# Gate/up integers in two DRAM tiles, stored by ScalarE, and subtracted in turn by VectorE and GpSimd

## The chip, the cores and the metric

The kernel runs on one core of a Trainium2 chip. The core has TensorE (PE, matrix multiplication), VectorE (DVE), ScalarE (ACT), GpSimd (POOL) and SyncE (SP, which mostly issues DMAs), and sixteen DMA engines that carry out what any of them issues. A DMA is issued by an instruction in the queue of one engine, and signals a semaphore when it has landed.

The metric is the time of one execution in device microseconds. Times are compared as medians of several executions. Line numbers such as L371 are lines of the kernel before the change.

## What is computed

Four layers are applied to 2 x 512 tokens of width 512, each as `x = x + layernorm(layer(layernorm(x)))`: a Mamba block (projections, a short convolution, a scan over 512 steps with 16 states for 1024 channels), a gated feed-forward layer whose weights are packed in 4 bits, an attention with one key and value head, and a feed-forward layer with latent experts. The change touches the unpacking of the second layer's weights. In the reference they are

```python
def dequant_gptq(qweight, scales, zeros, groupsize):
    K = qweight.shape[0] * PACK          # PACK = 8 nibbles along K
    q = qweight[k // PACK, :] >> (k % PACK * 4)[:, None] & 15
    z = zeros[:, n // PACK] >> (n % PACK * 4)[None, :] & 15
    zp = (z.astype(jnp.float32) + 1.0) * s
    return q.astype(jnp.float32) * s[g] - zp[g]        # g = k // 128
...
gate = x2 @ Wg                # 512 -> 1376
up = x2 @ Wu
inter = gate * jax.nn.sigmoid(gate) * up
out = (inter @ Wd).astype(jnp.float16)                 # 1376 -> 512
```

## The kernel before, in words

**Stages.** The two sequences are called batch 0 and batch 1. The Mamba scans of both batches fill the span up to about 566 us, with VectorE and GpSimd as the busy engines. Then come, in this order: the out-projection of batch 1 (`po`, L1334, 32 matmuls); the down-projection of batch 0's feed-forward layer (`fo`, L1353, 88 matmuls in 44 ticks, each with a weight pair `wd0_j` loaded from `wd_d`); then `gptq(1)`, the gate, up and down-projection of batch 1, beside which `chain(0)` (norm and attention of batch 0) runs; then the attention of batch 1 and the latent layer of both batches up to the end.

**Packed weights.** An int32 word of `gate_q` or `up_q` holds eight 4-bit numbers along the contraction dimension. Partition p of a tile holds one of 64 rows of words of gate (p below 64) or up, so that one nibble number j gives 128 rows of weights. For batch 0 the weights are fully dequantized during the scan (`wgu_d`). For batch 1 only the integers minus their zeros are made ("whole words") and written to a DRAM tile `wgi_d`; their scales `gus` are applied when the products leave PSUM, in `evict` of gptq.

**Whole words (L353 to L376).** The 1376 columns are cut at CUTS into 512, 512 and 352. For each cut and each j: VectorE takes the nibble out (L239), ScalarE casts the integers to float in place (L368), GpSimd subtracts the zeros (L370), SyncE stores the word (L371) into `wgi_d`, in the order "r a k n -> k r a n", so that the outermost of the destination's dimensions is k with 4 entries. The tile `q` has three buffers: the nibble of word k + 3 waits for the store of word k. The first two cuts are spawned 24 ticks into the stage; the third is spawned beside gptq(1).

**Weights from DRAM.** `gu_weights` (L391) loads `wg` and `wu` in strips of 256 columns from `wgi_d` through `w4` (L114). A load waits for the stores that wrote the columns it reads. `down_words` (L335) makes the weights of the down-projection and stores them to `wd_d`; `head_sums` (L378) sums the query weights over the heads.

**Norms.** `normed_job(i)` (L1280) takes the out-projection of token tile i of batch 1 through two layer norms, and asks TensorE for a transposition (`tp_f`, L1310) that is answered between matmuls of `fo`; `split` then makes the two parts `hhi` and `hlo` that gptq(1) multiplies.

**What sets the order.** `run(stream)` advances the stream that yields matmuls, and after each matmul one tick of all spawned jobs; a job that yields n sleeps for n ticks. The order of instructions on PE, ACT, DVE and POOL is pinned to the order in which they are made; the order of SyncE's queue is decided by the scheduler. The completion semaphores of DMAs of SyncE and ScalarE are eight lanes that are handed out in turn, and a DMA waits for the one before it on its lane. Consequently an instruction that waits holds everything behind it in its engine's queue.

Of the kernel before, what the change touches and what calls it, by code (L numbers as in the profile page):

```python
# [9 lines left out]
F32 = mybir.dt.float32  # L10
F16 = mybir.dt.float16
F32R = mybir.dt.float32r
I32 = mybir.dt.int32
# [6 lines left out]
P = 128  # L20
B = 2
S = 512
# [29 lines left out]
PW = 2 * P  # L52
NP = (INTER + PW - 1) // PW
CUTS = [(0, 2), (2, 4), (4, NP)]


@with_exitstack
def tile_sandwich(
# [129 lines left out]


    wgu_d = dram.tile([P, 2, KH, INTER], F32, tag="wgu", name="wgu_d")  # L190
    wgi_d = dram.tile([P, 2, KH, INTER], F32, tag="wgi", name="wgi_d")
    wd_d = dram.tile([INTER, H], F32, tag="wd", name="wd_d")
    wfe_d = dram.tile([P, KH, LAT], F32, tag="wfe", name="wfe_d")

# [43 lines left out]
    def nibble(q, qw, j):  # L238
        nc.vector.tensor_scalar(q, qw, 4 * j, 15, ALU.logical_shift_right, ALU.bitwise_and)  # L239

    class GateUpWords:
# [73 lines left out]
        def word(self, eng=nc.vector):  # L315
            for _ in self.steps(eng):
                pass
# [16 lines left out]
    def down_words(d, dq, loaded):  # L334

        nr = INTER // PACK
        m, hw = nr - P, H // 2
        qw, z, s, r, n = loaded
        wd_v = wd_d.rearrange("(r e) n -> e r n", e=PACK)
        for j in range(PACK):  # L340
            q = dq.tile([P, S], I32, tag="q", name=f"q_d{d}_{j}", bufs=2)
            nibble(q[:r, :n], qw[:r, :n], j)
            w = dq.tile([P, S], F32, tag="w", name=f"w_d{d}_{j}", bufs=3)
            nc.vector.tensor_sub(w[:r, :n], q[:r, :n], z[:r, :n])
            nc.gpsimd.tensor_mul(w[:r, :n], w[:r, :n], s[:r, :n])  # L345
            if d == 0:
                nc.sync.dma_start(out=wd_v[j, :P, :], in_=w[:, :H])
            else:
                for a in range(2):
                    nc.sync.dma_start(out=wd_v[j, P:nr, ts(a, hw)], in_=w[a * m : (a + 1) * m, :hw])  # L350
            yield 2 - j % 2

    def whole_words(a, iq):  # L353

        n0, n1 = CUTS[a][0] * PW, min(CUTS[a][1] * PW, INTER)
        n = n1 - n0
        qw = iq.tile([P, CW], I32, tag=f"qw{a}", name=f"qw_w{a}")
        z = iq.tile([P, CW], F16, tag=f"z{a}", name=f"z_w{a}")
        parts = [(i, src, 0, KH * RG, None, zd) for i, (src, zd) in enumerate(zip((gate_q, up_q), zds))]
        word_loads(parts, n0, n1, qw, z, None, 2, nc.sync, nc.sync)  # L360

        def words():
            for j in range(PACK):
                q = iq.tile([P, CW], I32, tag="q", name=f"q_w{a}_{j}", bufs=3)
                nibble(q[:, :n], qw[:, :n], j)
                yield 1
                w = q.bitcast(F32)
                nc.scalar.copy(w[:, :n], q[:, :n])  # L368
                yield 1
                nc.gpsimd.tensor_sub(w[:, :n], w[:, :n], z[:, :n])  # L370
                nc.sync.dma_start(  # L371
                    out=wgi_d[j * RG : (j + 1) * RG, :, :, n0:n1].rearrange("r a k n -> k r a n"),
                    in_=w[:, :n],
                )
                yield 1

        return words()

    def head_sums(dq):

        wqs = [(w48[:, k, 0:HD], Wq[ts(k, P)]) for k in range(KH)]
        wqs.append((b48[:, 0:HD], bq.partition_broadcast(P)))
        for i, (dst, src) in enumerate(wqs):
            wq = dq.tile([P, S], F32, tag="w", name=f"wq{i}", bufs=3).rearrange("p (d h) -> p d h", h=NH)
            nc.sync.dma_start(out=wq, in_=src)
            nc.vector.tensor_reduce(dst, wq, AX.X, ALU.add)
            yield 2
# [1 line left out]
    hTs, o16 = {}, {}  # L389

    def gu_weights(b, j):  # L391
        src = wgi_d if b else wgu_d
        cols = slice(j * PW, min((j + 1) * PW, INTER))
        n = cols.stop - cols.start
        return [w4(src[:, a, :, cols], f"w{nm}{b}_{j}", KH, n) for a, nm in enumerate("gu")]

# [55 lines left out]
    with ExitStack() as mamba:  # L452
# [261 lines left out]
        with ExitStack() as p2:  # L714
# [24 lines left out]
            def spawn(gen, lag=0):  # L739
                jobs.append([now[0] + lag, gen])  # L740
# [535 lines left out]
        with ExitStack() as p3:  # L1276
            dq = pool(p3, "dq2", 1)

            def normed_job(i, ps):

                name = f"mo1_{i}"
                o = new_u(f"o1_{i}")
                nc.scalar.copy(o, ps)
                yield 3
                mv = moments([o], name)
                rs = rstd(mv, name, 1)
                yield 2
                nm = minus_mean(mv, rs, name, 1)
                yield 1
                apply(o, o, rs, nm, 0)  # L1290
                yield 2
                nc.vector.tensor_add(xs(1)[i], xs(1)[i], o)
                name = f"f1_{i}"
                mv = moments([xs(1)[i]], name)
                rs = rstd(mv, name, 1)
                yield 2
                nm = minus_mean(mv, rs, name, 1)
                yield 1
                xn = jrow(f"xn_{name}")
                apply(  # L1300
                    xn.rearrange("p (k j r) -> p k r j", k=KH, j=PACK),
                    xs(1)[i].rearrange("p (k r j) -> p k r j", k=KH, j=PACK), rs, nm, 0,
                )
                yield 2
                tps = []

                def turn():
                    tp = bank(f"tp_f1_{i}").rearrange("p (k t) -> p k t", k=KH)
                    for kc in range(KH):
                        nc.tensor.transpose(tp[:, kc, :], xn[:, ts(kc, P)], ident)  # L1310
                    tps.append(tp)

                def split():
                    hi, lo = (t_[:, :, ts(i, P)] for t_ in hhl)
                    nc.scalar.copy(hi, tps[0])
                    yield 1
                    nc.vector.tensor_sub(lo, tps[0], hi.bitcast(F32))

                asks.append((turn, split()))

            def words_jobs():
                yield from down_words(0, dq, down[0])
                yield from down_words(1, dq, down[1])
                yield 20
                yield from head_sums(dq)

            def outs():
                po = [obank(f"po1_{i}") for i in range(TB)]
                for j in range(NCH // 2):
                    w = wo_pair(1, 0, j)  # L1330
                    tiles = [(e, i) for e in range(2) for i in range(TB)]
                    for e, i in sorted(tiles, key=lambda ei: ei[j == NCH // 2 - 1]):
                        c = 2 * j + e
                        nc.tensor.matmul(  # L1334
                            po[i], g[1][c][:, ts(i, P)], w[:, e, :],
                            start=(c == 0), stop=(c == NCH - 1),
                        )
                        yield
                        if c == NCH - 1:
                            spawn(normed_job(i, po[i]), 1)  # L1340
                for i, m in enumerate(IC):
                    j, e = divmod(i, 2)
                    if not e:
                        w = wst.tile([P, 2, H], F32, tag="w4", name=f"wd0_{j}")
                        n = len(IC[i : i + 2])
                        nc.sync.dma_start(
                            out=w[:m, :n],
                            in_=wd_d[i * P : i * P + n * m].rearrange("(k p) h -> p k h", p=m),
                        )
                    for t in range(TB):  # L1350
                        if not i:
                            fo0.append(obank(f"fo0_{t}"))
                        nc.tensor.matmul(  # L1353
                            fo0[t], its[i][:m, ts(t, P)], w[:m, e],
                            start=(i == 0), stop=(i == len(IC) - 1),
                        )
                        yield

            def whole_jobs():
                for words in whole[:2]:  # L1360
                    yield from words

            whole = [whole_words(a, iqp) for a in range(len(CUTS))]
            fo0 = []
            spawn(words_jobs(), 1)
            spawn(whole_jobs(), 24)
            run(outs())
            while jobs or asks:
                if asks:
                    answer()  # L1370
                tick()
            pin()
# [306 lines left out]
        yield from gptq_norm(b)  # L1679
        yield from attention(b, ask)  # L1680

    spawn(whole[2], 2)
    spawn(chain(0, fo0, lambda fn, then: asks.append((fn, then))), 1)
    run(gptq(1))
    while jobs or asks:
# [77 lines left out]
```

## Time and profile before

The median of three runs is 936.14 us.

| What | Before |
|---|---|
| Runs | 937.45, 933.98, 936.14 us |
| Profiled execution's own time | 933.81 us |
| Its span | 932.0 us |
| Mean granted TensorE clock | 0.964 |
| `q_w` nibbles on VectorE, 24 | 329 / 419 / 996 ns (min, median, max) |
| `q_w` casts on ScalarE, 24 | 474 / 617 / 624 ns |
| `q_w` subtracts on GpSimd, 24 | 856 / 1153 / 1273 ns |
| `wgi_d` store issues on SyncE, 24 | 511 / 524 / 573 ns, first at 596.3, last at 696.8 us |
| `po` on TensorE | 568.3 to 595.8 us |
| First gate matmul of gptq(1), `fg` | 661.12 us |

The span is the time between the first and the last instruction that the profiler saw; the execution's own time is a little longer. Each row of a group gives the number of instructions and the duration of one. In the waits, an engine's idle time is put down to what released it last; `DMA wgi_d<-q_w` is the store of a word's tile `q_w` into `wgi_d`, and `wg<-wgi_d` the load of a strip of it. In the chain of waits each row is a piece of time with its start, its length and the work that held it. The packets of section 3 of the page count the time of all sixteen DMA engines, so that a share of 25% is a quarter of their common time.

### The profile page before, as it was taken

How to read it: one execution, taken by the hardware profiler on the slowest of the kernel's cores; microseconds unless marked ns; L12 is line 12 of the kernel's file. 1: busy time of each engine (PE TensorE's matmuls, PEld its weight loads, DVE VectorE, ACT ScalarE, POOL GpSimd, SP SyncE). 2: the span in 40 equal slices, each digit the busy share in tenths (PEclk: the TensorE clock that was granted, in tenths of full speed). 3: DMA queues.
4: the chain of work that ended last, by engine and by line, in shares of the span. 5: the costliest groups of instructions: out<-in, count | busy, mean ns of one | idle time of the engine just before them, and what ended most of it. 6: DMA issues, size and time to landing. Idle time of an engine off the chain costs nothing. (4 is left out here: it accounts for less than half of the span.)

```text
span 932.0 us, 7483 instructions
## 1 busy us (share of the span) xinstructions
PE 828.5 (89%) x2188; PEld 383.7 (41%) x2188; DVE 729.6 (78%) x859; ACT 455.7 (49%) x706; POOL 535.6 (57%) x378
## 2 busy tenths in 40 slices
PE   6988978879999899599999998986589999999995
PEld 3433433333544443244444433342346545445442
DVE  6878899999999999999999997561485964535126
ACT  4357875656676656657565540242445554310110
POOL 7757796777887788867787876543353420011002
PEclk9998999899999999899999999999799999999998
DMA  6539011010003954101101024554442231101101
GB/s 202 202 138 378 29 38 39 30 38 31 23 24 98 319 204 145 60 0 46 45 23 46 8 88 168 183 203 149 127 122 87 70 114 46 68 12 41 39 0 45
DMA packets 48018, 86.82 MB, mean 93 GB/s; under 512 B 8134, under 2 KB 22833, under 8 KB 47978
## 3 DMA queue, kind: packets, MB, share of 16 engines
q1 hardware_dynamic: 45706, 80.35, 25.5%
q0 software_dynamic: 1984, 5.47, 1.6%
q10 hardware_dynamic: 288, 0.52, 0.2%
q8 instruction: 17, 0.28, 0.1%
q14 instruction: 23, 0.19, 0.1%
HBM read 69.45 MB, written 16.88 MB: 93 GB/s over the span
## 5 line engine op out<-in xcount | busy, mean ns | idle before, releaser
L1138 POOL TENSOR_TENSOR bx<-bx,C 128x1024 f32<-128x1024 f32 x128 | 302.4, 2363 | 100.5 <-DVE bx L1132 77.8
L1132 DVE TENSOR_TENSOR_SCAN bx<-da,bx 128x1024 f32<-128x1024 f32 x128 | 291.9, 2280 | 2.3 <-ACT da L1112 2.3
L1160 PE MATMUL py<-bx,ident 128*128 128x512 f32 x480 | 232.2, 613 | 27.4 <-POOL bx L1138 23.6
L1112 ACT ACTIVATE da<-dt,A 128x511 f32<-128x511 f32 x256 | 176.6, 690 | 148.9 <-DVE bx L1132 144.4
L1128 DVE TENSOR_TENSOR bx<-du,B 128x1024 f32<-128x1024 f32 x127 | 153.1, 1206 | 2.6 <-DMA B<-scr 0.5
L1160 PEld LDWEIGHTS py<-bx,ident 128*128 128x128 f32 x480 | 91.3, 196 | 151.1 <-issue 96.4
L130 POOL TENSOR_TENSOR rs_lo<-ve_lo,mhalf 128x1 f32<-128x1 f32 x8 | 7.4, 919 | 91.4 <-DVE ve_lo L128 91.4
L780 PE MATMUL pg<-xT,w_g 128*128 128x512 f32 x114 | 56.0, 621 | 3.3 <-ACT dt L598 3.3
L1602 PE MATMUL pup<-hT_l,wup 128*128 128x512 f32 x128 | 57.7, 606 | 0.0
L1666 PE MATMUL pd<-wdn,hid 128*128 128x512 f32 x128 | 55.9, 597 | 0.0
L368 ACT CAST q_w<-q_w 128x512 f32<-128x512 int32 (+1 forms) x24 | 13.7, 572 | 76.3 <-DVE q_w L239 75.2
L1353 PE MATMUL fo<-wd,it 128*128 128x512 f32 (+1 forms) x88 | 42.8, 639 | 7.0 <-DMA wd<-wd_d 5.2
L370 POOL TENSOR_TENSOR q_w<-q_w,z_w 128x512 f32<-128x512 f32 (+1 forms) x24 | 26.3, 1096 | 39.1 <-ACT q_w L368 36.2
L1442 PE MATMUL fo<-wd,pg 128*128 128x512 f32 (+1 forms) x88 | 44.2, 594 | 0.3 <-DVE pg L1456 0.3
L1052 PE MATMUL fg<-hT_f,wg 128*128 128x512 f32 (+1 forms) x88 | 42.5, 594 | 0.0
L1052 PE MATMUL fu<-hT_f,wu 128*128 128x512 f32 (+1 forms) x88 | 40.4, 594 | 1.4 <-ACT dt L598 1.4
L510 DVE SCALAR_TENSOR_TENSOR u<-px,ch,u 128x511 f32<-128x511 f32 (+2 forms) x48 | 35.9, 747 | 6.5 <-ACT u L503 5.4
L1666 PEld LDWEIGHTS pd<-wdn,hid 128*128 128x128 f32 x128 | 24.8, 193 | 31.5 <-issue 31.0
L1602 PEld LDWEIGHTS pup<-hT_l,wup 128*128 128x128 f32 x128 | 24.6, 196 | 29.2 <-issue 29.2
L1619 DVE TENSOR_TENSOR hid<-hid 128x512 f32<-128x512 f32 x16 | 11.0, 689 | 32.6 <-ACT hid L1618 32.5
L1481 PE MATMUL fg<-hhi,wg 128*128 128x512 f32 (+1 forms) x44 | 24.1, 549 | 13.7 <-DMA wg<-wgi_d 10.9
L780 PEld LDWEIGHTS pg<-xT,w_g 128*128 128x128 f32 x114 | 22.1, 198 | 33.3 <-issue 28.4
(256 smaller groups left out, 1312.3 us busy)
## 6 DMA issues: line engine op xcount, KB each, us to landing
wo<-in_W_outT SPq DMA_DIRECT2D x20, 512.0 KB
B<-scr SPq DMA_DIRECT2D x16, 512.0 KB
C<-scr SPq DMA_DIRECT2D x16, 512.0 KB
w_x<-in_W_in SPq DMA_DIRECT2D x8, 512.0 KB
wgu_d<-w_gu POOLq DMA_DIRECT2D x16, 256.0 KB, 2.5
w_g<-in_W_in SPq DMA_DIRECT2D x8, 512.0 KB
wgi_d<-q_w SPq DMA_DIRECT2D x16, 256.0 KB
wup<-in_up_w SPq DMA_DIRECT2D x8, 512.0 KB
```

Of the source, the lines that this page charges most:

```text
L510: nc.vector.scalar_tensor_tensor(uc[:, s:], ps[:, : S - s], ch[:, c, KCONV - 1 - s : KCONV - s], uc[:, s:], ALU.mult, ALU.add,)
L780: nc.tensor.matmul(ps, w[:, k, ts(e, P)], xT[b][:, k, :], start=(k == 0), stop=(k == KH - 1))
L1052: nc.tensor.matmul(ps[:m], wt[j][a][:, kc, e * P : e * P + m], hT[:, kc, :], start=(kc == 0), stop=(kc == KH - 1),)
L1112: nc.scalar.activation(das[s % 2][:, i, 1:], st["dt", b, c][:, 1:], AF.Exp, scale=A[:, c, n : n + 1])
L1128: nc.vector.tensor_mul(bx, st["du"].unsqueeze(1).to_broadcast([P, NG, S]), Bbs[b][gi])
L1132: nc.vector.tensor_tensor_scan(flat, das[s % 2].rearrange("p n t -> p (n t)"), flat, 0.0, ALU.mult, ALU.add)
L1138: nc.gpsimd.tensor_mul(bxs[s], bxs[s], Cbs[b][s % NGI])
L1160: nc.tensor.matmul(st["y"], ident, bx[:, i, :], start=False, stop=last)
L1353: nc.tensor.matmul(fo0[t], its[i][:m, ts(t, P)], w[:m, e], start=(i == 0), stop=(i == len(IC) - 1),)
L1442: nc.tensor.matmul(fo[t], its[i][:m, ts(t, P)], w[:m], start=(i == 0), stop=(i == len(IC) - 1),)
L1602: nc.tensor.matmul(ps, w[:, kc, ts(e, P)], src[kc], start=(kc == 0), stop=(kc == KH - 1))
L1666: nc.tensor.matmul(pd, hid[kc][:, ts(i, P)], wdn[kc], start=(kc == 0), stop=(kc == INT // P - 1),)
```

## The change

The 1376 columns are cut into two, of 1024 and 352 columns, and each has a DRAM tile of its own in place of the one `wgi_d`. A word is now a job of its own. Words with even j are subtracted by VectorE, which also turns them into floats, so that they need no cast; those with odd j are cast by ScalarE and subtracted by GpSimd as before. All stores are issued by ScalarE. Words of the first tile are spawned every three ticks and those of the second every two, from tick 22 on, and none is left for the time of gptq(1). The `q` tile still has three buffers, now of 1024 columns. The `w` tile of the down and query weights has five buffers in place of three. In `normed_job` the distances of 2 become 4 or 3.

```diff
+WHOLE = [(0, 4 * PW), (4 * PW, INTER)]
...
-    wgi_d = dram.tile([P, 2, KH, INTER], F32, tag="wgi", name="wgi_d")
+    wgi_d = [
+        dram.tile([P, 2, KH, n1 - n0], F32, tag=f"wgi{n0}", name=f"wgi{n0}_d") for n0, n1 in WHOLE
+    ]
...
-            w = dq.tile([P, S], F32, tag="w", name=f"w_d{d}_{j}", bufs=3)
+            w = dq.tile([P, S], F32, tag="w", name=f"w_d{d}_{j}", bufs=5)
...
-        def words():
+        def word(j):
+            q = iq.tile([P, WHOLE[0][1]], I32, tag="q", name=f"q_w{a}_{j}", bufs=3)[:, :n]
+            nibble(q, qw, j)
+            w = q.bitcast(F32)
+            if j % 2:
+                yield 2
+                nc.scalar.copy(w, q)
+                yield 2
+                nc.gpsimd.tensor_sub(w, w, z)
+                yield 3
+            else:
+                nc.vector.tensor_sub(w, q, z)
+                yield 2
+            nc.scalar.dma_start(
+                out=wgi_d[a][j * RG : (j + 1) * RG].rearrange("r a k n -> k r a n"), in_=w,
+            )
+
+        def words(pace):
             for j in range(PACK):
-                q = iq.tile([P, CW], I32, tag="q", name=f"q_w{a}_{j}", bufs=3)
-                nibble(q[:, :n], qw[:, :n], j)
-                yield 1
-                w = q.bitcast(F32)
-                nc.scalar.copy(w[:, :n], q[:, :n])
-                yield 1
-                nc.gpsimd.tensor_sub(w[:, :n], w[:, :n], z[:, :n])
-                nc.sync.dma_start(
-                    out=wgi_d[j * RG : (j + 1) * RG, :, :, n0:n1].rearrange("r a k n -> k r a n"),
-                    in_=w[:, :n],
-                )
-                yield 1
+                spawn(word(j))
+                yield pace
...
     def gu_weights(b, j):
-        src = wgi_d if b else wgu_d
         cols = slice(j * PW, min((j + 1) * PW, INTER))
+        src = wgu_d
+        if b:
+            n0 = WHOLE[j // 4][0]
+            src, cols = wgi_d[j // 4], slice(cols.start - n0, cols.stop - n0)
...
                 mv = moments([o], name)
                 rs = rstd(mv, name, 1)
-                yield 2
+                yield 4
                 nm = minus_mean(mv, rs, name, 1)
                 yield 1
                 apply(o, o, rs, nm, 0)
-                yield 2
+                yield 3
...
-                for words in whole[:2]:
-                    yield from words
-
-            whole = [whole_words(a, iqp) for a in range(len(CUTS))]
+                for words, pace in zip(whole, (3, 2)):
+                    yield from words(pace)
+
+            whole = [whole_words(a, iqp) for a in range(len(WHOLE))]
...
-            spawn(whole_jobs(), 24)
+            spawn(whole_jobs(), 22)
...
-    spawn(whole[2], 2)
     spawn(chain(0, fo0, lambda fn, then: asks.append((fn, then))), 1)
```

The second half of `normed_job` changes in the same way: its two distances of 2 become 4 and 3.

More of the change, by code (lines that the diff above doesn't have):

```diff
@@ L353, in whole_words @@
     def whole_words(a, iq):
-        n0, n1 = CUTS[a][0] * PW, min(CUTS[a][1] * PW, INTER)
+        n0, n1 = WHOLE[a]
         n = n1 - n0
-        qw = iq.tile([P, CW], I32, tag=f"qw{a}", name=f"qw_w{a}")
-        z = iq.tile([P, CW], F16, tag=f"z{a}", name=f"z_w{a}")
+        qw = iq.tile([P, n], I32, tag=f"qw{a}", name=f"qw_w{a}")
+        z = iq.tile([P, n], F16, tag=f"z{a}", name=f"z_w{a}")
         parts = [(i, src, 0, KH * RG, None, zd) for i, (src, zd) in enumerate(zip((gate_q, up_q), zds))]
         word_loads(parts, n0, n1, qw, z, None, 2, nc.sync, nc.sync)
-        def words():
-            for j in range(PACK):
-                q = iq.tile([P, CW], I32, tag="q", name=f"q_w{a}_{j}", bufs=3)
-                nibble(q[:, :n], qw[:, :n], j)
-                yield 1
-                w = q.bitcast(F32)
-                nc.scalar.copy(w[:, :n], q[:, :n])
-                yield 1
-                nc.gpsimd.tensor_sub(w[:, :n], w[:, :n], z[:, :n])
-                nc.sync.dma_start(
-                    out=wgi_d[j * RG : (j + 1) * RG, :, :, n0:n1].rearrange("r a k n -> k r a n"),
-                    in_=w[:, :n],
-                )
-                yield 1
-        return words()
+        def word(j):
[15 more added lines that the diff above has]
+        def words(pace):
+            for j in range(PACK):
+                spawn(word(j))
+                yield pace
+        return words
     def head_sums(dq):
@@ L383, in head_sums @@
         for i, (dst, src) in enumerate(wqs):
-            wq = dq.tile([P, S], F32, tag="w", name=f"wq{i}", bufs=3).rearrange("p (d h) -> p d h", h=NH)
+            wq = dq.tile([P, S], F32, tag="w", name=f"wq{i}", bufs=5).rearrange("p (d h) -> p d h", h=NH)
             nc.sync.dma_start(out=wq, in_=src)
@@ L1295, in normed_job @@
                 rs = rstd(mv, name, 1)
-                yield 2
+                yield 4
                 nm = minus_mean(mv, rs, name, 1)
@@ L1303, in normed_job @@
                 )
-                yield 2
+                yield 3
                 tps = []
```

## The prediction

> **What bounds the kernel now.** I read the page's head first, then the waits of the stretch that the diff touches (580 to 700 us), then the chain of waits inside it, then what the DMA engines did, then the windows by stage.
>
> ```profile
> PE 828.5 (89%) x2188; PEld 383.7 (41%) x2188; DVE 729.6 (78%) x859; ACT 455.7 (49%) x706; POOL 535.6 (57%) x378
> ```
>
> TensorE is busy for 89% of the span, so time can come only from its gaps. The waits of 580 to 700 us (engine, line, what it waited for: total, times, longest) show the largest gap beside the words:
>
> ```profile
> ACT q_w L368 <- DVE q_w L239: 75.2, 16, 38.5
> ...
> DVE q_w L239 <- DMA wgi_d<-q_w: 23.5, 9, 3.7
> ...
> PE fg L1481 <- DMA wg<-wgi_d: 10.9, 1, 10.9
> ```
>
> TensorE waits 10.9 us for the first load of gate/up integers, and VectorE's nibbles wait 23.5 us for stores to free a q tile. No engine is late with arithmetic: a store is. The chain of waits from 626 to 664 us says the same:
>
> ```profile
> 631.09 8.01 DMA wgi_d<-q_w
> ...
> 639.19 0.44 DVE q_w L239
> ...
> 639.65 0.63 ACT q_w L368
> ...
> 640.34 1.17 POOL q_w L370
> ...
> 641.53 7.82 DMA wgi_d<-q_w
> ...
> 652.41 8.58 DMA wg<-wgi_d
> ...
> 661.12 2.91 PE fg L1481 x6
> ```
>
> A word's arithmetic is 0.44 + 0.63 + 1.17 = 2.2 us, its store 8 us with three in flight: 3 x 262 KB in 8 us is 98 GB/s. Why so slow? The DMA view of 635 to 638 us, when nothing but these stores was in flight, then that of 581 to 584 us (packets, MB, share of 16 engines):
>
> ```profile
> q1 hardware_dynamic: 137, 0.27, 24.9%
> ...
> wgi_d<-q_w SPq DMA_DIRECT2D x2, 256.0 KB
> ```
>
> ```profile
> q1 hardware_dynamic: 555, 1.01, 93.6%
> ...
> wd_d<-w_d SPq DMA_DIRECT2D x2, 256.0 KB
> ```
>
> Stores to wgi_d occupy a quarter of the sixteen engines, those to wd_d nearly all. The first have 4 as outermost size of their destination (k of "k r a n"). So these stores have about 96 GB/s, 24 on each of four engines (89 / 4 = 22 and 412 / 16 = 26, in the windows below, bound it).
>
> ```profile
> 76.00:86.00 10.00, 10.00 (x19) 4.05 (x18) 7.91 (x6) 8.35 (x16) 9.42 (x6) 0.76 1.03 412
> ...
> 635.00:638.00 3.00, 1.67 (x3) 0.82 (x4) 0.43 (x1) 0.62 (x1) 1.29 (x2) 0.85 0.25 89
> 661.00:700.00 39.00, 31.73 (x100) 18.42 (x101) 32.53 (x62) 21.92 (x37) 20.05 (x18) 0.96 0.36 100
> 700.00:762.00 62.00, 61.11 (x230) 37.07 (x230) 43.11 (x73) 35.56 (x58) 21.41 (x16) 1.00 0.30 96
> ```
>
> (Window, length, busy time of PE, PEld, DVE, ACT, POOL, clock, DMA share, GB/s.) In gptq(1), 661 to 700 us, TensorE is idle 39 - 31.7 = 7.3 us; afterwards 0.9 us. Those 7.3 and the 10.9 are what this change can win.
>
> **Checking that view on the time before.** Through the four engines, from the first store (596.3) to the landing of wg_0 (661.0), went 16 stores, 4.19 MB / 96 = 43.7 us; a sixteenth per engine of the loads issued in between (four pairs of wd, five wq, four wd, five wdn, gam, bet: 5.96 MB / 16 / 24 GB/s = 15.5); wg_0's own part, 0.5 MB / 16 / 24 = 1.4. That is 60.6 for a measured 64.7: a factor of 1.07 for gaps.
>
> **The change part by part.** *Words, wider and all ahead of gptq(1).* Tile 0 holds the bytes of cuts 0 and 1, with 4 still outermost: 43.7 us again. The other 352 columns, before stored in gptq(1), are 1.44 MB, 180 KB a word, 1.9 us each. By the program's order, wg_0 now waits for all of tile 0 and, through shared completion semaphores, for words 0' and 2' of the second tile: 3.75 us. SP issues wg_0 behind every load of the stage, and wd_0, wd_1 and three wdn, which went out before the first store, now come behind it (the pair wd_0 stood at 589.0 and now stands after the last wd_d store, issued near 594): 7.80 MB / 16 / 24 = 20.3 instead of 15.5. The sum is 43.7 + 3.75 + 20.3 = 67.8 us; at the 26 GB/s of the bus's best window it is 62.6, with the factor 1.07 it is 72.4.
>
> *Start of the stores.* The words start two ticks earlier (22 for 24; 0.86 us each: the 32 matmuls of po take 568.3 to 595.8), and word 0 goes nibble, subtract, store, without cast and POOL. A 1024-column nibble I put at 0.7 (0.42 for 512, 0.34 for 352), the VectorE subtract at 1.25 (L344, the same operation on 512, takes 0.69 alone and 1.29 in the mean; L1128, 1024 columns, 1.21). Five w buffers spare VectorE some 3 us of waits for wd_d stores under po. First store near 593 instead of 596.3, bounds 592 and 595.
>
> *When gptq(1) begins.* 593 + 67.8 = 661 for the landing of 2', 665.4 with the factor. Only then may wg_0 be issued; before it stood queued from 652.4 on. Issue is 0.5 us and landing 3.5 (an estimate between 0.52 MB at the 338 GB/s of the second DMA view, 1.6, and the chain's 8.58). So fg starts between 661 and 670; I take 668.5, near the upper end because the factor was measured in this very stretch: 7.4 late on 661.1.
>
> *The queues the stores move to.* Stores now stand in ScalarE's order, 16 issues of 0.52 us (L371's median). Queued behind each are hhi copies and, at the end, gptq's first evictions (L1463), for which TensorE's banks wait. The last words, 5' and 7', need a q tile freed by 1' and 3': three more 1.9 us stores after 2', then nibble, cast, POOL and issue, 0.4 + 0.5 + 0.9 + 0.5: near 8 us after 2', where the first eviction would be ready after 0.5 + 3.5 + 1.3 = 5.3. That is 2.5 more (0 to 5). VectorE's nibbles 6 to 4' wait for stores in front of the norm operations and of hlo, so the four transposes, which share TensorE's ticks with fo, come late. With a store landing every 5.5 us from 599 on, the last one falls near 643; 20 of fo's 44 ticks of 0.87 us follow it: 660, still ahead of wg_0.
>
> The Trainium skill's page "DMA: Bandwidth & Descriptors", in its section "Issuing engines are not separate DMA queues", speaks against the move: DMAs of every issuing engine run on the same sixteen engines, so another issuer saves issue time alone, here at most 16 x 0.52 = 8 us of a queue that is not the bound. Its section "Why a DMA increments its semaphore by 16 and not by 1" says that the number of engines is the largest k up to 16 that divides the outermost size of both sides: 4 here, as the 24.9% shows, and unchanged by wider words. Were a row of 1024 columns to spread over sixteen engines, tile 0 would cost 11 us and not 43.7.
>
> *What is taken out.* From 661 to 700 us go eight nibbles (3.6 us of VectorE, 32.5 of 39 busy), eight casts (3.9) and eight POOL subtracts (7.8). VectorE ends most of TensorE's waits there, so I credit 4 us; at least 2, at most the 7.3 of idle time. POOL's half of the subtracts and SP's 27 instructions fewer are worth nothing: behind each stands a store; if that cover were gone they would be worth the 1.2 us per word that the chain shows.
>
> *Longer norm distances.* Six ticks more for each of four norms (2 + 1 twice), 5.2 us, hidden behind the stores: the last transpose falls near 643, the stores end past 660. Uncovered, the last norm would delay fo by those 5.2 us.
>
> **Sum.** +7.4 + 2.5 - 4 = +5.9 us: the profiled execution's 933.8 (span 932.0) would become 939.7. That execution lies 2.3 below the median of 936.1, so on the median's scale 942.0. Ends of this case: -0.1 + 2 - 4 with the early start, +9 + 4 - 2: 934 to 947.
>
> **Rivals.** *Gptq wins more than the start loses* (0.15). The factor is smaller because 4 KB rows move better, as the 412 GB/s window suggests: fg starts at 662.5, the front of words costs 0, and all 7.3 us of idle time go: 936.1 + 1.4 - 7.3 = 930. Against it: TensorE also waits there for evictions of its own.
>
> *The four engines are not the bound* (0.10). The 10.9 us come from wg_0 being queued late on SP, and TensorE's own tail decides: fo, started near 600.6 (wd_0 issued near 594.7 and some 6 us to land) and with 44 ticks of 0.87 and the waits for transposes, ends near 646 to 650 and fg follows: -11 - 4, 921. For it: wg_0 is issued at 652.4 only. Against it: the 24.9%.
>
> *Loss and gain cancel* (0.12): fg starts at 663, gain 4 and front 2: 936.
>
> *Norms locked behind words* (0.13), the same sign and worse: each VectorE nibble that waits for a store holds a norm, the transposes slip by one store period of 524 KB / 96 = 5.5 us each, fo ends past 672, and fg starts at 676: 936.1 + 15 + 2.5 - 4 = 950. It decides from the point where tp_f of the last norm passes 655.
>
> **How the numbers follow.** The forecast's case has 0.50, of which its lower end, 0.05, lies within the bound. About 0.5% of 936, 4.7 us, is what a measurement can tell from no change: faster is below 931.5, slower above 940.8. Faster: 0.15 + 0.10 = 0.25. Same: 0.12 + 0.05 = 0.17. Slower: 0.45 + 0.13 = 0.58. The time is the likeliest case's, 942; its own range is 934 to 947. The range that leaves out the 921 of the second rival and what lies beyond the 950 of the last is 926 to 953.
>
> **What would show it.** Right: in the new profile the stores of the first tile hold a quarter of the engines, 524 KB per 5.5 us; SP's wg_0 is issued on the landing of a store after 660; fg's first wait is over 15 us; idle time in gptq(1)'s first 39 us falls from 7.3 to about 3. Wrong: a DMA share well above a quarter while only these stores run, or fg before 655, or a last tp_f after 655.

## The result and the profile after

The changed kernel takes 945.54 us (median of four runs, 945.16 to 947.04) against 935.06 us of the kernel before on the same chip (931.7 to 937.45). The ratio is 1.0118 with a 95% interval of 1.0082 to 1.0153: slower by about 1.2%. Its profiled execution took 945.69 us, 11.9 more than the one shown before.

Line numbers in a view are those of the kernel that it shows. The head of the page and the waits of all engines from 575 to 715 us (engine, line, what it waited for: total, times, longest), kernel after:

```profile
PE 831.8 (88%) x2188; PEld 385.1 (41%) x2188; DVE 735.3 (78%) x859; ACT 449.4 (48%) x690; POOL 520.5 (55%) x362
```

```profile
DVE q_w L242 <- DMA wgi_d<-q_w: 49.5, 13, 6.5
...
PE fo L1366 <- DMA wd<-wd_d: 13.3, 2, 12.7
...
PE tp_f L1323 <- ACT xn_f L154: 9.7, 2, 7.9
...
PE fg L1494 <- ACT pg L1476: 8.7, 1, 8.7
...
PE fg L1494 <- DMA wg<-wgi_d: 2.7, 1, 2.7
```

TensorE has as many instructions as before and is busy for 3.3 us more (831.8 for 828.5), so 8.6 of the 11.9 us are idle time. VectorE waits 49.5 us for stores to free a q tile, where it was 23.5. The wait of 10.9 us for wg has nearly gone from TensorE's list (2.7 us), though not because the load comes earlier: other things are late too. fo waits for its first weights and then for transposes, so that it ends at 665 us, just ahead of wg's landing; and after three banks TensorE waits 8.7 us for the first eviction. The chain of waits from 595 to 690 us (start, length, what held it):

```profile
592.93 11.64 DMA wgi_d<-q_w
...
631.53 12.70 DMA wgi_d<-q_w
...
645.99 14.63 DMA wgi_d<-q_w
...
661.15 5.24 DMA wgi_d<-q_w
...
666.92 7.85 DMA wgi_d<-q_w
...
675.24 0.49 ACT q_w L371
...
675.86 0.86 POOL q_w L373
676.74 0.53 ACTq L378
...
677.79 0.70 ACT pg L1476
...
678.53 1.22 PE fg L1494 x2
```

Two thirds of this chain are stores of words. The last link is new (a prime marks a word of the second tile): nibble 7' waits for the store that went out at 666.92, its cast, subtract and issue follow, and only behind them in ScalarE's queue stands the first eviction (677.79), for which TensorE's fourth bank waits. In the DMA view of 655 to 660 us the stores of both tiles have this share of the sixteen engines:

```profile
q10 hardware_dynamic: 161, 0.44, 22.9%
q1 hardware_dynamic: 28, 0.05, 2.6%
```

The wider words, in another queue, still fill a quarter of the engines at 88 GB/s. Two windows of gptq(1), from the first fg on and past the wait for the first eviction (columns as before):

```profile
668.00:707.00 39.00, 27.59 (x84) 16.32 (x85) 27.77 (x55) 16.29 (x26) 11.78 (x11) 0.82 0.31 96
679.00:718.00 39.00, 35.36 (x117) 20.79 (x117) 31.57 (x58) 21.36 (x33) 14.86 (x12) 0.95 0.26 80
```

Counted from the first fg, TensorE is idle for 11.4 of 39 us, where it was 7.3. Past the wait, the first 39 us of undisturbed matrix work have 3.6 us of idle time. That is the part in which the change gains.

Landmarks tell the account. The stage begins (first po) at 568.8 instead of 568.3 us: +0.5. The first fg is at 667.9 instead of 661.1, +6.3 beyond that. From the first fg to the first fu (the up matmul) it takes 11.7 instead of 3.5 us: +8.2. The rest of the span is 3.1 us shorter. Together 11.9.

### The profile page after: what moved, and what is told of

It reads as the page before. It is cut to its first block, busy times and chain, and to the rows that moved or that the text cites. A ratio compares the mean times of both kernels' runs of the same rounds, so it can differ in the third digit from the quotient of the medians.

```text
span 943.9 us, 7392 instructions
## 1 busy us (share of the span) xinstructions
PE 831.8 (88%) x2188; PEld 385.1 (41%) x2188; DVE 735.3 (78%) x859; ACT 449.4 (48%) x690; POOL 520.5 (55%) x362
## 5 line engine op out<-in xcount | busy, mean ns | idle before, releaser
L1366 PE MATMUL fo<-wd,it 128*128 128x512 f32 (+1 forms) x88 | 43.9, 655 | 13.3 <-DMA wd<-wd_d 13.3
L242 DVE TENSOR_SCALAR q_w<-qw_w 128x1024 int32<-128x1024 int32 (+1 forms) x16 | 9.6, 604 | 49.5 <-DMA wgi_d<-q_w 49.5
L373 POOL TENSOR_TENSOR q_w<-q_w,z_w 128x1024 f32<-128x1024 f32 (+1 forms) x8 | 12.4, 1556 | 39.0 <-ACT q_w L371 39.0
```

Of the source, the lines that this page charges most:

```text
L1366: nc.tensor.matmul(fo0[t], its[i][:m, ts(t, P)], w[:m, e], start=(i == 0), stop=(i == len(IC) - 1),)
```

## The experiments

Each ratio in brackets is against the kernel before on the same chip, whose medians there were 933.61 to 937.5 us. Waits and distances are those of one profiled execution of each kernel.

**1. The layout of the stores, in both kernels.** The tile is laid out so that a word's 128 partitions become the outermost size of its store. The strips' loads keep 128 outermost, and the transposed x takes its columns in natural order to match.

```diff
-        dram.tile([P, 2, KH, n1 - n0], F32, ...) for n0, n1 in WHOLE
+        dram.tile([P, PACK, n1 - n0], F32, ...) for n0, n1 in WHOLE
...
-                out=wgi_d[a][j * RG : (j + 1) * RG].rearrange("r a k n -> k r a n"), in_=w,
+                out=wgi_d[a][:, j], in_=w,
...
+            src = src.rearrange("(a k r) j n -> (r j) a k n", a=2, k=KH)
...
-                apply(
-                    xn.rearrange("p (k j r) -> p k r j", k=KH, j=PACK),
-                    xs(1)[i].rearrange("p (k r j) -> p k r j", k=KH, j=PACK), rs, nm, 0,
-                )
+                apply(xn, xs(1)[i], rs, nm, 0)
```

(In the loading of the packed words, the partitions of gate and up become halves instead of alternating, for the same reason.) On the kernel before:

> The kernel before, with wgi_d laid out so that a word's 128 partitions are the outermost size of its store (and the strips' loads still have 128 outermost); nothing else is moved. Theory (the four DMA engines bound the stage): a store lands in under 4 us and not in 8, VectorE's 23.5 us of waits for stores vanish, fg starts at 646 to 651 instead of 661, where fo ends, and the time falls by 10 to 15 us, to 920 to 926. Rival (the load wg_0 is late for its place in SyncE's queue, whatever the stores take): fg within 3 us of 661 and the time within 4 us of the kernel before.

On the changed kernel:

> The changed kernel with the same layout in both tiles. Theory (its loss is the four engines): both terms of the loss go, fg starts at 646 to 652, no bank waits for an eviction behind a word, and the time is 917 to 925. Rival (the loss is in ScalarE's order and in the longer norms): fg at 660 or later and the time above 935.

Measured: 915.71 us for the kernel before with this layout (ratio 0.9778, 0.9725 to 0.9831) and 908.35 us for the changed one (0.9722, 0.967 to 0.9774). Both beat both kernels. The waits of VectorE and TensorE of the first, in 575 to 700 and 560 to 700 us:

```profile
DVE q_w L239 <- DMA wgi_d<-q_w: 7.0, 5, 2.0
```

```profile
PE fg L1480 <- DMA wg<-wgi_d: 1.1, 1, 1.1
```

The store waits fall from 23.5 to 7.0 us, and the 10.9 us wait for wg to 1.1. From the first po to the first fg it takes 75.0 us instead of 92.8. The DMA view of the second from 595 to 596 us, when one of these stores was alone in flight, and that from 600 to 640 us:

```profile
q10 hardware_dynamic: 98, 0.40, 100.6%
```

```profile
q1 hardware_dynamic: 4756, 8.09, 56.6%
q10 hardware_dynamic: 1872, 4.75, 30.7%
```

A store alone now holds all sixteen engines, where it held 24.9% before. Loads and stores together use 87% of them in 600 to 640 us, at 12.84 MB / (87.3% of 640 engine-microseconds) = 23 GB/s an engine, as before: there are more engines, not faster ones. The first theory is shown, and its size was underrated: 18 us where 10 to 15 were expected on the kernel before, and 37 us on the changed one, over three times its loss. A small part may come from elsewhere, since the natural order of x also shortens four norm operations on ScalarE (L153, 1.26 us each before, 0.81 now). The rule of the Trainium skill's page "DMA: Bandwidth & Descriptors" (section "Why a DMA increments its semaphore by 16 and not by 1": the outermost sizes choose the number of engines) agrees with these shares.

**2. The stores back on SyncE.**

```diff
-            nc.scalar.dma_start(
+            nc.sync.dma_start(
                 out=wgi_d[a]...
```

> The changed kernel with the stores issued by SyncE again. Theory (the words' casts stand in ScalarE's order and wait for stores, whoever issues them, and the four engines stay full): the time stays within 4 us of 945.5, TensorE still waits over 5 us for the first evictions. Rival (the issues in ScalarE's queue are what holds the evictions): fg as in the changed kernel, the wait for evictions gone, 935 to 938.

Measured: 946.67 us (940.89 to 947.82; ratio 1.0114). The time is as the theory had it, but the place is not: TensorE now waits 9.2 us for wg (first fg 107.6 us after the first po, where it was 99.1) and no longer for evictions. The strips' loads then stand behind the last stores in SyncE's queue, as the evictions do in ScalarE's. In the changed kernel, who issues only chooses who is held. The time, by the ratio 1.0114 beside 1.0118, agrees with the Trainium skill's page "DMA: Bandwidth & Descriptors", section "Issuing engines are not separate DMA queues", by which another issuer saves issue time alone.

**3. The second tile's words beside gptq(1).**

```diff
-                for words, pace in zip(whole, (3, 2)):
-                    yield from words(pace)
+                yield from whole[0](3)
...
+    spawn(whole[1](6), 2)
     spawn(chain(0, fo0, ...
```

> The changed kernel with the second tile's words spawned beside gptq(1), as the third cut was before. Theory (+6.8 at the start of fg of which 3.75 x 1.07 are the words 0' and 2', +8.2 in front of the first evictions, -3 gained later): fg near 664, the 8.7 us wait for evictions gone, the gain gone too, 936 to 941. Rival (the second tile has no part in it): 944 to 947.

Measured: 945.56 us (941.83 to 946.24; ratio 1.0106), which misses the expected 936 to 941. The trace shows why. The wait for the first eviction is gone (2.6 us from the first fg to the first fu), and wg is there in time, but fg still begins 100.4 us after the first po, because fo ends then:

```profile
PE fo L1366 <- DMA wd<-wd_d: 17.7, 2, 12.7
PE tp_f L1323 <- ACT xn_f L154: 8.3, 1, 8.3
```

(TensorE's waits, 560 to 700 us.) And gptq(1), from the first fg to its last fo, takes 104.6 us (4.1 of them a wait for a strip); in the kernel before it is 100.1. So fo is a second bound of nearly the same length as the words, which taking words out doesn't move.

**4. The last layer's loads taken out of the stage.**

```diff
-                nc.sync.dma_start(out=t_, in_=down_w[ts(kc, P), :])
+                nc.gpsimd.dma_start(out=t_, in_=down_w[ts(kc, P), :])
...
-            nc.sync.dma_start(out=gam, in_=ln_gamma.partition_broadcast(P))
-            nc.sync.dma_start(out=bet, in_=ln_beta.partition_broadcast(P))
+            nc.gpsimd.dma_start(out=gam, in_=ln_gamma.partition_broadcast(P))
+            nc.gpsimd.dma_start(out=bet, in_=ln_beta.partition_broadcast(P))
```

> The changed kernel, but the ten 256 KB loads of the last layer (wdn, gam, bet) are issued by GpSimd at their place in the program, after gptq(1), and no longer by SyncE beside the stores. Theory (each load takes a sixteenth of its bytes from each of the four full engines: 2.62 MB / 16 / 24 GB/s = 6.8 us, with the factor 7.3): word 7 of the first tile lands 5 to 8 us earlier against the end of po, fo and fg start earlier, fg by 2 to 7 us, and the time is 939 to 943. Rival (loads on sixteen engines cost the stores nothing): word 7 lands within 2 us of the changed kernel's, 944 to 947.

Measured: 939.57 us (ratio to the kernel before 1.0066, 1.0043 to 1.0088), 6 us less than the changed kernel (5 by the ratios). The last word's store goes out 102.9 us after the first po instead of 107.9, wg_0 is issued 90.1 instead of 93.8 us after it, and fg begins after 95.3 instead of 99.1. Loads on sixteen engines do take a share of the four; 3.7 to 5.0 us came of the 6.8 that were estimated.

On the wide layout the same edit:

> The changed kernel with the wide layout and the ten last loads issued by GpSimd after gptq(1). Theory (on sixteen engines the stores no longer bind, so taking 2.62 MB of loads out of the stage brings little): 905 to 910. Rival (the DMA engines at 90% between 600 and 630 us are the bound even so): the wait for wd_0 gone and 900 to 905.

Measured: 909.93 us (907.51 to 912.6; ratio 0.9728) beside 908.35 (0.9722), with 3.5 us of wait for wd_0 left. No gain from these loads is seen there any more.

**5. GpSimd as the issuer, in the kernel before.**

```diff
-                nc.sync.dma_start(
+                nc.gpsimd.dma_start(
                     out=wgi_d[j * RG : (j + 1) * RG, ...
```

> The kernel before with the stores of the words issued by GpSimd, same pattern. Theory of this study (4 as outermost size means four engines; a GpSimd-issued DMA may take another four each time): if the four rotate, the DMA share with three stores in flight is over 40%, a store lands in 4 us or less, fg starts before 653 and the time is 920 to 927. Rival (the pattern's rows or the memory are slow, or the same four engines are used): 8 us a store and 932 to 940.

Measured: 929.9 us (0.9937, 0.9909 to 0.9965), between the two theories. The DMA view of 637 to 640 us:

```profile
q0 software_dynamic: 356, 0.29, 42.3%
q1 hardware_dynamic: 50, 0.09, 7.7%
```

These stores hold 42%, more than four of sixteen engines, but move 0.29 MB in 42.3% of 48 engine-microseconds, 14 GB/s an engine, where SyncE's had 0.27 / (24.9% of 48) = 23. A store still took some 8 us, and the sixteenth goes out 58.1 us after the first (601.4 to 659.5), in the kernel before 55.5 (596.3 to 651.8): the stores are no faster. Yet fg begins 78.6 us after the first po (92.8 before). The rows of the first load of a strip, wg_0, in SyncE's timeline show why, first in the kernel before, then in this run, with the eleventh store in GpSimd's timeline of this run:

```profile
651.77 0.53 SPq L371 DMA_DIRECT2D wgi_d<-q_w  x1
652.41 0.52 SPq L114 DMA_DIRECT2D wg<-wgi_d  x1
```

```profile
639.55 0.37 SPq L114 DMA_DIRECT2D wg<-wgi_d  x1
```

```profile
641.14 0.71 POOL L371 DMA_DIRECT2D wgi_d<-q_w  x1 [0.30 <-DMA wgi_d<-q_w]
```

wg_0 reads columns of the first cut alone, which eight stores write. In the kernel before it stood in SyncE's queue behind the sixteenth store; here it goes out ahead of the eleventh. TensorE then waits 7.9 us for an eviction, so that 14 us at fg are worth 5 in the time. The queue was thus a second bound of the kernel before. In the changed kernel wg_0 reads the tile of 1024 columns and needs all eight of its words, whoever issues them. That more engines help with this pattern is not shown; why an engine moves less for GpSimd's DMAs stays open, and so does which engines they were.

**6. Three w buffers.**

```diff
-            w = dq.tile([P, S], F32, tag="w", name=f"w_d{d}_{j}", bufs=5)
+            w = dq.tile([P, S], F32, tag="w", name=f"w_d{d}_{j}", bufs=3)
```

> The changed kernel with three w buffers for the down weights and query weights, as before the change. Theory (five buffers spare VectorE some waits; the stores are the bound): the first word's store comes 1 to 3 us later, fg and the end 0 to 3 us later, 945 to 949. Rival (five buffers put the loads wd_0 and wd_1 behind all wd_d stores and so delay fo, which decides): fo starts 5 us earlier and the time is 938 to 942.

Measured: 944.63 us (943.47 to 949.22; ratio 1.0125), just under the theory's range. The five buffers do delay fo: with three, wd_0 is there in time and fo begins 1.7 us after po's last matmul begins, where it is 13.3. But what fo gains it loses at the transposes (TensorE waits 22.6 us for xn_f instead of 9.7), and fg begins 98.2 us after the first po. The transposes wait for norms, and these stand on VectorE and ScalarE behind words that wait for stores: in this run's chain, the store of 619.94 us takes 12.55, and only behind it come a nibble, a subtract and the norm, up to the first xn_f at 634.57. With the wide layout:

> The changed kernel with the wide layout and three w buffers. With the stores no longer the bound, fo's start after po is what five buffers can touch: TensorE waits 4.1 us there for wd_0 in the run with five. If the buffers cause it, the wait is under 1.5 us and the time 904 to 907; if not, 908 to 911.

Measured: 910.65 us (907.81 to 914.52; ratio 0.9754). The wait for wd_0 is gone, as it was to be if the buffers cause it, but the time that was to come with that did not: a wait of 3.2 us for the first norm came in its place, and fg begins 75.2 us after the first po instead of 74.8.

**7. The short norm distances.** The distances 4 and 3 become 2 again.

```diff
-                yield 4
+                yield 2
                 nm = minus_mean(mv, rs, name, 1)
...
-                yield 3
+                yield 2
```

> The changed kernel with the norm distances of before. Theory (the norms stand behind nibbles that wait for stores, and fg waits for wg_0 behind the stores): fg against the end of po within 2 us of the changed kernel's 72.0, the time 943 to 947. Rival (six ticks a norm hold the transposes and fo): the last transpose 4 to 6 us earlier, and as much of it as fo decides, 2.7 us, in the time: 940 to 943.

Measured: 949.35 us (944.8 to 951.23; ratio 1.0138). fg begins 99.1 us after the first po, exactly as with the long ones. So the longer distances cost nothing up to fg, as both the prediction and this theory had it; the time above the range has two places: the first po is 3.3 us later (572.1 against 568.8), before anything that this edit touches, and the wait for the first eviction is 11.0 instead of 8.7. Together with three buffers on the wide layout:

> The changed kernel with the wide layout, three w buffers and the norm distances of before. Theory (with the stores off the path, TensorE's own ticks bound the stage, and its last gaps are the 4.1 us for wd_0, gone with three buffers, and 3.2 us for the last norm, gone with short distances): fg 70 to 72.5 us after the start of po instead of 75, the time 903 to 908. Rival (the gaps move elsewhere): 74 us or more after po, 908 to 913.

Measured: 916.86 us (910.54 to 919.78; ratio 0.9802), above the ranges of both, and fg 77.5 us after the first po. This theory fell: with short distances the way to fg took 2.3 us more (77.5 against 75.2), in one execution of each.

**8. The front of gptq(1): order or bandwidth.**

```diff
                 nc.gpsimd.tensor_sub(w, w, z)
-                yield 3
+                yield 1 if a else 3
```

> The changed kernel, but an odd word of the second tile yields 1 and not 3 before its store, so that on ScalarE store 3' stands ahead of cast 5' and no longer behind it. Theory (store 3' was ready at 662.6 us and was held until 666.9 by cast 5', which waited for store 1' in ScalarE's order; nibble 7' and so the first eviction wait for its landing): store 3' goes out within 1.5 us of its subtract, TensorE's wait for the first eviction falls from 8.7 to 1 to 4.5 us, fg itself stays 98 to 101 us after the start of po, and the time is 939 to 943. Rival (the front is the four engines' time for the last stores and the strips' loads, whatever the order): the wait stays at 7 us or more, 944 to 948.

Measured: 942.91 us (941.53 to 946.5; ratio 1.0075). In the changed kernel, store 3' went out only behind cast 5' (ScalarE's timeline; the last row covers two stores, 3' and 6'):

```profile
666.86 0.48 ACT L371 CAST q_w<-q_w 128x352 f32<-128x352 int32 x1 [4.56 <-DVE q_w L242]
666.92 4.36 ACTq L378 DMA_DIRECT2D wgi_d<-q_w  x2
```

Here ScalarE's and then VectorE's timeline (3' with its neighbour, and the nibble 7' that waits for its landing):

```profile
663.28 1.18 ACTq L378 DMA_DIRECT2D wgi_d<-q_w  x2
```

```profile
672.38 0.34 DVE L242 TENSOR_SCALAR q_w<-qw_w 128x352 int32<-128x352 int32 x1 [2.63 <-DMA wgi_d<-q_w]
```

The store goes out 3.6 us earlier, but nibble 7' comes only 2.5 us earlier (672.38 for 674.87), and TensorE still waits 8.1 us. The time falls into the theory's range, its mechanism does not hold: order has little of the front, which leaves most of it to the rival, bandwidth. The first fu comes 108.7 us after the first po instead of 110.8; fg comes 1.2 us earlier too, so order is worth 2 us of the 8 at most, and between the first fg and the first fu 0.9 (10.8 for 11.7).

## Why the prediction was right or wrong

**Right: the bound and the start.** The four engines were named from a share of 24.9%, and the layout alone is worth 18 us in the kernel before. (The view of 581 to 584 us, read as stores to wd_d alone, also had a load of 256 KB in flight; experiment 1 carries the reading without it.) The first store was put at 593 us and went out at 592.9. Word 2' was to land between 661 and 665.4; wg_0, which waits for it, was issued at 662.64. fg was put at 668.5 and began at 667.9: the term of +7.4 measured +6.8, of which 0.5 had come in before po. That fit is in part luck. From 592.9 to 662.6 us are 69.7, where the sum was 67.8 and with the factor of 1.07 it was 72.4: the factor needed was 1.03. From its issue to fg, wg_0 then took 5.3 us and not 4.0, and the two errors point opposite ways. The shares of the loads, the less plain part of that sum, experiment 4 shows, at 3.7 to 5.0 us for an estimated 6.8.

Two of the prediction's signs of being right did not come. fg's first wait was to be over 15 us and was 2.7, because fo ended only at 665.3. The idle time of gptq(1)'s first 39 us was to fall to about 3; it rose to 11.4, of which the wait for the first eviction is 8.7, and is 3.6 only past that wait.

**Wrong in size: the front.** "That is 2.5 more (0 to 5)" measured 8.2, outside its own bounds. The step took 1.9 us for each of the three stores after 2', as if nothing else used the four engines. But wg_0, wu_0 and the next wg were issued at that very time (662.64, 666.44, 666.90): 1.57 MB, and 1.57 / 16 / 24 GB/s = 4.1 us more, an estimate that no run tests by itself. The prediction counts this share for every load ahead of wg_0 and leaves it out for wg_0 and what follows it. Experiment 8 puts at most another 2 us to store 3' standing behind cast 5'.

**Right in size: what is taken out.** The credit was 4 us within 2 to 7.3. The landmarks give 3.1. On the wide layout, where nothing else disturbs it, gptq(1) takes 95.7 us with no words beside it and 100.1 with them: 4.4.

**Wrong, without deciding: fo.** It was to start near 600.6 and end near 660. It began at 609.2 and ended at 665.3, 2.6 us ahead of fg. The five w buffers, costed as a saving of 3 us for VectorE (experiment 6: the first store 24.1 us after the first po, with three buffers 28.8), put wd_0 behind all stores of wd_d in SyncE's queue: issue at 598.6, not "near 594", and some 10 us to land beside the stores. Had the words been a little faster, fo would have decided; in experiment 3 it did.

**The total.** +5.9 was forecast and +11.9 came in the profiled executions, +10.5 in the medians, within the range of 926 to 953. Of the difference of 6.0, the front is 5.7, the smaller gain 0.9 and the 0.5 before po are added, and the start takes 1.1 off.

**The rivals.** That the four engines are not the bound fell with experiment 1; but its premise, that wg_0 is late for its place in SyncE's queue, holds for the kernel before (experiment 5), beside the four engines. That gptq wins more than the start loses fell with the front. That norms are locked behind words is half true: the last transpose began at 647, not past 655, so fo came close to deciding and did not. What stays open is the spread of 6.7 us in the place of the first po (566.0 to 572.7 us in these kernels, whose scans are the same): differences of a few microseconds between two kernels' times are read here from distances within the stage.

## What to carry to other kernels

Look at the share of the DMA engines in a stretch where one kind of transfer is alone: a share of a quarter pointed here to a layout that confines it. Changing the outermost size was worth 18 and 37 us, while no change of issuer, buffers, loads or order was worth more than 6. While the stores were confined, a sum over those few engines, with the sixteenth of every other transfer in it, gave the landing of a word within 2 to 3 us, provided that the transfers that the landing itself releases are counted too. Work moved ahead of a stage must have landed before the stage's first in-order instruction, else, as here, it only changes which engine is held: SyncE's loads or ScalarE's evictions. So ask of a late load both when its data land and what stands ahead of it in its queue.

## What the runs showed that was not expected

The wide layout also shortens the issue. The median of a store's issue, in the kernel after and in the same kernel with the wide layout (engine, tile, count: min/median/max in ns, first and last start):

```profile
L378 ACTq DMA_DIRECT2D wgi_d<-q_w x16: 515/526/1102, 592.9 to 676.7; - x16
```

```profile
L378 ACTq DMA_DIRECT2D wgi_d<-q_w x16: 326/326/374, 594.0 to 641.5; - x16
```

The same bytes in the same number of rows take 326 ns to issue instead of 526. And the change itself, slower by 1.2% on the old layout, has the lower time of the two on the new one, 908.35 against 915.71 us (their intervals against the kernel before overlap, so that a gain is not shown; gptq(1) alone is 4.4 us shorter in the profiled executions): what the edit costs depends on what bounds the stage.
